# Conv stage in phases a step apart, 512-byte rows, gates in the combine: a two-layer convolution network on one NeuronCore

## Chip, cores and metric

The kernel runs on one core of a Trainium2 chip. The time is the device time of one execution in microseconds; the lower, the better. Times are given as the median of several runs. A profile is one more execution, recorded by the hardware profiler; its span runs from the first instruction to the last.

## The reference

The input x is 32 images of 128 channels and 56 x 56 pixels, float32. Two layers follow one another. What matters, cut from the reference:

```python
# layer 0: depthwise 7x7 conv, layernorm over channels, top-2 of 8 experts with capacity
x = conv_general_dilated(input, dw_kernel, (1, 1), ((3, 3), (3, 3)), feature_group_count=C) + dw_bias
x = transpose(x, (0, 2, 3, 1))
x = (x - mean) / sqrt(var + 1e-06) * ln_gamma + ln_beta      # over the 128 channels of a token
xf = x.reshape(T, C)                                         # T = 32*56*56 = 100352 tokens
topv, topi = top_k(xf @ Wg + bg, 2);  wts = softmax(topv)
order = argsort(-wts[:, 0])                                  # who gets a slot: sure tokens first
cap = int(1.25 * T / 8);  keep = pos < cap                   # 15680 slots per expert
h = gelu(einsum('ecd,edf->ecf', eb, W1) + b1)                # eb: the rows gathered into slots
y = einsum('ecf,efd->ecd', h, W2) + b2
contrib = y[slot] * gate;  moe = sum of a token's two contribs
x = input + x_skip + layer_scale * moe                       # x_skip = the normalised x
# layer 1: dilated 3x3 conv to 64 channels, gelu, 2-D FFT, attention over 8x8 channel blocks
# and a channel gate in frequency space, two inverse FFTs, absolute values, plus x
```

## The kernel before

A token is a pixel. Tokens are kept as 784 columns of 128 partitions: one column is two patches of 8 x 8 pixels, one of an image of the first half and one of the second. The program is written with a tile framework that gives out buffers, sets all semaphores and lays out the order of each engine's queue itself, by priority (the order of the program) and by what its model thinks is ready; each engine then runs its queue strictly in that order.

**Conv stage** (lines 114 to 286). Eight groups g of four images (two image pairs) each, 98 token columns a group. `conv(g, y)` gives 16 steps of eight channels: two loads on SP (xt, 784 KB; wt, 448 KB; three buffers each), 32 matrix products, and two VectorE evictions that add the bias and write y, a tile of 98 columns by 131 numbers (`ROW`: 128 channels, two gates, the first expert's number). There are two buffers of y. The evictions have two forms: L150 goes through the output token by token, L157 channel by channel. `norm(g, y)` gives seven steps of 14 columns and then `choose()`. A step takes the sum over channels (L172), the squares with an accumulator on ScalarE (L177, a column each), the root (L181) and reciprocal (L182), then two VectorE operations a column (L185, L188) that subtract the mean, scale, and apply gamma and beta in place; then TensorE transposes the columns four at a time (L196), ScalarE copies them out (L198), and a product per column with Wg (L200; the column is the stationary operand, Wg has 8 columns) gives the logits. `choose()` takes the two largest of eight logits for the 98 columns, the softmax, the sort key, writes the gates and the expert's number into the last three numbers of each row of y (L256 to L258), and issues seven stores of y to xf in DRAM on SP (L269, 917 KB each). The loop at L274 puts a norm step of group g-1 behind every second conv step of group g; the conv of group g+2 writes into the y buffer that group g's stores read.

**Selection and experts** (L305 to L684). A threshold on the key is found per expert by 24 bisections (count, L352), then lists of token numbers are made. `fetch` gathers 512 rows of xf (L585, GpSimd, 128 rows at a time, 524 bytes each), transposes them (L591), and works out each row's gate from its last three numbers with three small VectorE operations (L596, L604). `expert` does the two products (L619, L627) with Gelu between; VectorE adds the bias (L638), multiplies by the gate (L644), and SP stores the rows to yf.

**Layer 1** (L690 to the end). `layer1_input` prepares a pair of images in seven steps: load the normalised rows from xf (L738), gather each token's two expert rows from yf with 14 GpSimd gathers (L742, into four buffers of seven columns), add them (L748, twice), transpose, and add into the padded input (L758). The first pair is prepared before the loop; the steps of every further pair are put between the parts of the pair before by `ahead()`. In the loop: the 3x3 convolution (L837), Fourier transforms as pairs of transposes (L780, copied by VectorE, L781) and products (L793, L981), the attention weights (L872 to L894), the attention (L901 to L914) and the gate.

Of the kernel before, what the change touches and what calls it, by code (L numbers as in the profile page):

```python
# [55 lines left out]
ROW = C + 3  # L56
# [15 lines left out]
def conv_seq_kernel(ctx: ExitStack, tc: tile.TileContext, t: dict, out: bass.AP, dbg: dict):  # L72
# [9 lines left out]
    route = ctx.enter_context(tc.tile_pool(name="route", bufs=1))  # L82
    dram = ctx.enter_context(tc.tile_pool(name="dram", bufs=1, space=DRAM))
# [17 lines left out]
    xf = dram.tile([J * 128, ROW], F32, name="xf")  # L101
# [3 lines left out]
    slot1 = route.tile([128, J], I32, name="slot1")  # L105
    slot2 = route.tile([128, J], I32, name="slot2")
# [6 lines left out]

    with tc.tile_pool(name="a1", bufs=1) as a1, tc.tile_pool(name="a2", bufs=2) as a2, tc.tile_pool(
# [5 lines left out]
        wg = load(a1, "wg", [C, E], t["Wg"])  # L120
        bgB = load(a1, "bgB", [128, E], rowbc(t["bg"], 128))
        revi = load(a1, "revi", [128, E], rowbc(t["revi"], 128))
        TG = 2 * NP
        TC = 2 * NB

        def conv(g, y):


            def step(c0):
                xt = a3.tile([PK, CB, 4 * NCB * NB], F32, name="xt")  # L130
                nc.sync.dma_start(out=xt, in_=t["x8"][g, c0 // CB])
                wt = a3.tile([PK, CB, 2, P8 * P8], F32, name="wt")
                nc.sync.dma_start(out=wt, in_=t["wt"][c0 // CB])
                xv = xt.rearrange("k c (h n q) -> k c h n q", h=2, n=2)
                for c4 in range(0, CB, 4):
                    ps = bank("psa")
                    for c in range(4):
                        for b in range(2):
                            for h in range(2):
                                nc.tensor.matmul(  # L140
                                    ps[h * 64 : (h + 1) * 64, c * TG : (c + 1) * TG],
                                    lhsT=wt[:, c4 + c, b, :],
                                    rhs=xv[:, c4 + c, h, :, b * NB : b * NB + NP],
                                    start=(b == 0),
                                    stop=(b == 1),
                                )
                    yo = y[:, :, c0 + c4 : c0 + c4 + 4]
                    bias = dwbB[:, c0 + c4 : c0 + c4 + 4]
                    if c4 == 0:
                        nc.vector.tensor_tensor(  # L150
                            out=yo,
                            in0=ps[:, : 4 * TG].rearrange("p (c t) -> p t c", c=4),
                            in1=bias.unsqueeze(1).broadcast_to([128, TG, 4]),
                            op=ALU.add,
                        )
                    else:
                        nc.vector.tensor_tensor(  # L157
                            out=yo.rearrange("p t c -> p c t"),
                            in0=ps[:, : 4 * TG].rearrange("p (c t) -> p c t", c=4),
                            in1=bias.unsqueeze(2).broadcast_to([128, 4, TG]),  # L160
                            op=ALU.add,
                        )

            return [lambda c0=c0: step(c0) for c0 in range(0, C, CB)]

        def norm(g, y):

            lg = a2.tile([128, TG, E], F32, name="lg")

            def step(t0):  # L170
                s1 = a4.tile([128, TC], F32, name="s1")
                nc.vector.tensor_reduce(out=s1, in_=y[:, t0 : t0 + TC, :C], axis=AX.X, op=ALU.add)  # L172
                nc.vector.tensor_scalar(out=s1, in0=s1, scalar1=-1.0 / C, scalar2=None, op0=ALU.mult)  # L173
                ss = a4.tile([128, TC], F32, name="ss")
                for i in range(TC):
                    sq = a4.tile([128, C], F32, name="sq")
                    nc.scalar.activation(  # L177
                        sq, y[:, t0 + i, :C], AF.Square, bias=s1[:, i : i + 1], accum_out=ss[:, i : i + 1]
                    )
                sd = a4.tile([128, TC], F32, name="sd")  # L180
                nc.scalar.activation(sd, ss, AF.Sqrt, scale=1.0 / C, bias=eps6)  # L181
                nc.vector.reciprocal(sd, sd)  # L182
                for i in range(TC):
                    yi = y[:, t0 + i, :C]
                    nc.vector.scalar_tensor_tensor(  # L185
                        out=yi, in0=yi, scalar=s1[:, i : i + 1], in1=gB, op0=ALU.add, op1=ALU.mult
                    )
                    nc.vector.scalar_tensor_tensor(  # L188
                        out=yi, in0=yi, scalar=sd[:, i : i + 1], in1=bB, op0=ALU.mult, op1=ALU.add
                    )  # L190
                pl = bank("pl")
                for i0 in range(0, TC, 4):
                    ni = min(4, TC - i0)
                    pt = bank("pyt")
# [80 lines left out]
        for g in range(HI // 2):  # L275
            y = a2.tile([128, TG, ROW], F32, name="y")
            steps = conv(g, y)
            for i, step in enumerate(steps):
                step()
                if i % 2 and behind:  # L280
                    behind.pop(0)()
# [850 lines left out]
```

## Time and profile before

| what | value |
|---|---|
| time, median of 3 runs | 6373.91 us (6367.38 to 6375.63) |
| profiled execution | 6380.61 us, span 6378.8 us |
| TensorE, VectorE, ScalarE, GpSimd busy | 5121.9, 3203.4, 2190.9, 2595.7 us |
| conv stage | 0 to 1427 us |
| selection | 1427 to about 1724 us |
| experts | to about 3713 us |
| filling of layer 1 (first pair gathered) | to about 3880 us |
| layer 1, 16 pairs | to 6378.8 us |
| all DMA traffic | 622.42 MB |

A busy time is the sum over the engine's instructions without overlap. The share of a whole span says little here, since the five stages have different limits: what a change in a stage is worth is read from that stage's windows and from the chain of work that ended last, which is followed back from the last instruction. In the rows by line, "out<-in" are the program's tiles, the first number is the busy time, the second the mean length of one instruction, and behind the bar stands the engine's idle time in front of these instructions and what ended it. One matrix product in float32 shows as two passes, a transpose as one.

### The profile page before, as it was taken

To read this page: it belongs to the slowest core of one execution; us is meant where nothing else is said; L and a number is where in the kernel's file an instruction comes from. 1 tells how busy PE (TensorE), PEld (TensorE's weight loads), DVE (VectorE), ACT (ScalarE), POOL (GpSimd) and SP (SyncE) were. 2 spreads that over 40 slices of the span, in tenths; PEclk is the share of its full clock that TensorE was granted. 3 is DMA by queue.
4 is the path that set the end of the run, shared out by engine and by line. 5 is a ranking of instruction groups with operands and counts; after the bars stand their busy time and mean duration, and the time that the engine had idled before them with its cause. 6 is when DMAs were issued, how large, how long until landed. Compare 5 with 4: busy or idle time off the path is not lost.

```text
span 6378.8 us, 88000 instructions
## 1 busy us (share of the span) xinstructions
PE 5121.9 (80%) x33610; PEld 3637.3 (57%) x33610; DVE 3203.4 (50%) x7090; ACT 2190.9 (34%) x4455; POOL 2595.7 (41%) x2556
## 2 busy tenths in 40 slices
PE   7777877740299999999999937888888888888887
PEld 6666776630167667677777723555555555555554
DVE  4566665559753553553544323444444444444443
ACT  1333332330033333333333313444444444444444
POOL 0000000000154454454454457666666666666640
PEclk8666666655599999999999968888888899888888
DMA  7677776550022222222222243444444444444431
GB/s 206 149 168 161 158 159 155 118 95 23 12 69 66 65 66 69 64 68 68 66 66 67 69 119 73 108 107 106 106 107 107 106 108 106 105 107 106 108 91 26
DMA packets 515495, 622.42 MB, mean 98 GB/s; under 512 B 65529, under 2 KB 439810, under 8 KB 510978
## 3 DMA queue, kind: packets, MB, share of 16 engines
q1 hardware_dynamic: 433410, 448.14, 27.5%
q0 software_dynamic: 81664, 168.65, 12.4%
q8 instruction: 266, 4.36, 0.3%
q14 instruction: 155, 1.27, 0.1%
HBM read 448.37 MB, written 168.19 MB: 97 GB/s over the span
## 4 chain that ended last, share of the span: by engine, by line
PE 49%; DVE 14%; POOL 11%; issue 9%; DMA 8%; ACT 5%; SPq 3%; DVEq 0%; POOLq 0%; ACTq 0%
PE pf L837 12%; PE py L627 8%; POOL xg L585 7%; PE ph L619 6%; PE psa L140 5%; POOL y L742 5%; PE pl L200 4%; PE pm L793 3%; DVE junk L352 3%; SPq L269 3%; DMA xg<-xf,ids 2%; PE pyt L196 2%; PE pt L780 2%; DMA xf<-y 2%; DMA y<-yf,slot 1%
## 5 line engine op out<-in xcount | busy, mean ns | idle before, releaser
L585 POOL DMA_INDIRECT xg<-xf,ids x984 | 979.4, 995 | 2690.9 <-DVE ids L557 1720.4
L742 POOL DMA_INDIRECT y<-yf,slot x1568 | 1616.1, 1031 | 879.6 <-issue 433.9
L622 ACT ACTIVATE hT<-ph,b1t 128x512 f32<-128x512 f32 (+1 forms) x992 | 675.6, 682 | 1290.1 <-PE ph L619 1263.6
L627 PEld LDWEIGHTS py<-W,hT 128*128 128x128 f32 x7872 | 940.1, 192 | 220.8 <-issue 107.3
L627 PE MATMUL py<-W,hT 128*128 128x128 f32 x7872 | 987.1, 279 | 44.4 <-DVE yo L638 41.9
L619 PE MATMUL ph<-xT,W 128*128 128x512 f32 (+1 forms) x1984 | 886.5, 589 | 0.0
L837 PE MATMUL pf<-xp,cw 128*64 128x448 f32 x4032 | 782.1, 541 | 0.0
L140 PE MATMUL psa<-xt,wt 112*64 112x98 f32 x8192 | 556.9, 306 | 50.6 <-DMA wt<-in_wt_dram 49.9
L619 PEld LDWEIGHTS ph<-xT,W 128*128 128x128 f32 x1984 | 358.5, 191 | 348.6 <-issue 344.4
L140 PEld LDWEIGHTS psa<-xt,wt 112*64 112x64 f32 x8192 | 509.0, 178 | 73.3 <-issue 38.5
L837 PEld LDWEIGHTS pf<-xp,cw 128*64 128x64 f32 x4032 | 276.1, 135 | 444.8 <-issue 437.4
L596 DVE SCALAR_TENSOR_TENSOR gat<-xg 128x4 f32<-128x4 f32 (+2 forms) x256 | 42.2, 165 | 942.9 <-DMA xg<-xf,ids 942.1
L177 ACT ACTIVATE sq<-y,s 128x128 f32<-128x128 f32 x784 | 303.5, 391 | 284.6 <-DVE s L173 284.6
L748 DVE TENSOR_TENSOR xs<-xs,y 128x896 f32<-128x896 f32 x224 | 244.2, 1090 | 287.1 <-DMA y<-yf,slot 150.2
L196 PE MATMUL pyt<-ident,y 128*128 128x128 f32 x784 | 187.7, 371 | 235.2 <-DVE y L150 117.9
L200 PE MATMUL pl<-wg,yT 128*128 128x8 f32 x1568 | 326.8, 335 | 59.2 <-ACT yT L198 58.9
L200 PEld LDWEIGHTS pl<-wg,yT 128*128 128x128 f32 x1568 | 308.4, 291 | 111.3 <-ACT yT L198 93.5
L781 DVE COPY F<-pt 112x512 f32<-112x512 f32 x112 | 77.2, 690 | 511.6 <-PE pt L780 511.0
L198 ACT COPY yT<-pyt 128x512 f32<-128x512 f32 x224 | 118.5, 531 | 626.6 <-PE pyt L196 613.3
L844 ACT ACTIVATE feat<-pf,bn_shift,bn_scale 128x448 f32<-128x448 f32 x112 | 81.1, 724 | 703.9 <-PE pf L837 703.3
L196 PEld LDWEIGHTS pyt<-ident,y 128*128 128x128 f32 x784 | 137.3, 201 | 260.8 <-issue 126.3
L781 DVE COPY T<-pt 116x512 f32<-116x512 f32 (+3 forms) x368 | 234.3, 651 | 93.1 <-PE pt L780 91.2
(516 smaller groups left out, 7093.1 us busy)
## 6 DMA issues: line engine op xcount, KB each, us to landing
xt<-in_x_dram SPq DMA_DIRECT2D x128, 784.0 KB
yf<-yo SPq DMA_DIRECT2D x240, 256.0 KB
xp<-in_xp_dram SPq DMA_DIRECT2D x32, 1832.0 KB
wt<-in_wt_dram SPq DMA_DIRECT2D x128, 448.0 KB
xf<-y SPq DMA_DIRECT2D x56, 917.0 KB
xs<-xf SPq DMA_DIRECT2D x112, 448.0 KB
y<-yf,slot POOLq DMA_INDIRECT x1568
out_dram<-oa SPq DMA_DIRECT2D x224, 112.0 KB
```

The source lines that it names most:

```text
L140: nc.tensor.matmul(ps[h * 64 : (h + 1) * 64, c * TG : (c + 1) * TG], lhsT=wt[:, c4 + c, b, :], rhs=xv[:, c4 + c, h, :, b * NB : b * NB + N ...
L177: nc.scalar.activation(sq, y[:, t0 + i, :C], AF.Square, bias=s1[:, i : i + 1], accum_out=ss[:, i : i + 1])
L196: nc.tensor.transpose(pt[:, i * 128 : (i + 1) * 128], y[:, t0 + i0 + i, :C], ident)
L200: nc.tensor.matmul(pl[:, (i0 + i) * E : (i0 + i + 1) * E], lhsT=yT[:, i * 128 : (i + 1) * 128], rhs=wg, start=True, stop=True,)
L585: nc.gpsimd.indirect_dma_start(out=xg[:n, q, :], out_offset=None, in_=xf, in_offset=bass.IndirectOffsetOnAxis(ap=ids[:n, c0 + q : c0 + q + ...
L619: nc.tensor.matmul(ph[:, :ns], lhsT=W1[:, e, f * C : (f + 1) * C], rhs=xT[:, :ns], start=True, stop=True)
L622: nc.scalar.activation(hT[:, f, :ns], ph[:, :ns], AF.Gelu, bias=b1t[:, e, f : f + 1])
L627: nc.tensor.matmul(py[:n, q * C : (q + 1) * C], lhsT=hT[:, f, q * 128 : q * 128 + n], rhs=W2[:, e, f, :], start=(f == 0), stop=(f == FF // ...
L742: nc.gpsimd.indirect_dma_start(out=y[:, m, :], out_offset=None, in_=yf, in_offset=bass.IndirectOffsetOnAxis(ap=s[:, j0 + m : j0 + m + 1], ...
L748: nc.vector.tensor_tensor(out=xs, in0=xs, in1=y, op=ALU.add)
L781: copy(to[:, i0 : i0 + ni, :].rearrange("p i c -> p (i c)"), pt[: to.shape[0], : ni * 128],)
L837: nc.tensor.matmul(pf[i * DD : (i + 1) * DD, : 8 * W], lhsT=cw[:, k, :], rhs=xps[i][:, o : o + 8 * RP].rearrange("p (h w) -> p h w", w=RP) ...
```

## The change

It rewrites the conv stage and moves the gates.

- Rows of xf are 128 numbers, 512 bytes. The gates are kept in SBUF (`gates`, two tiles of 128 x 784) and no longer travel with the rows; the expert's number is not stored.
- Normalisation runs in blocks of 16 columns (six, and one of two). A block has five phases: `stats` (bn_stats per column on VectorE, seven small operations and one Sqrt), `norm` (one ScalarE Identity per column with a scale and a bias per partition, in place; then gamma and beta on VectorE for the whole block, and the block's store to xf, issued on ScalarE's queue), `across` (transposes and copies), `logits` (Wg, padded to 32 columns, as the stationary operand, and 512 tokens streamed; the four groups of four columns write four quarters of the partitions of one bank; a ScalarE copy), `back` (four transposes, and the bias).
- The phases of a block stand one conv step apart, and blocks start at steps 0, 1, 3, 4, 6, 7 and 9 of the next group's 16; `choose` follows at step 14 and issues no stores.
- All evictions have the token-by-token form.
- `fetch` and `expert` lose the gate operations; the combine multiplies each gathered tile of seven columns by its gate, on VectorE, before adding it.
- slot1 and slot2 are allocated after the conv stage.

```diff
-    xf = dram.tile([J * 128, ROW], F32, name="xf")
+    xf = dram.tile([J * 128, C], F32, name="xf")
+    gates = [route.tile([128, J], F32, name=f"gate{r}") for r in (1, 2)]
...
-                    if c4 == 0:
-                        nc.vector.tensor_tensor(
-                            out=yo,
...
+                nc.vector.tensor_tensor(
+                    out=y[:, :, cs],
+                    in0=ps[:, : 4 * TG].rearrange("p (c t) -> p t c", c=4),
+                    in1=dwbB[:, cs].unsqueeze(1).broadcast_to([128, TG, 4]),
+                    op=ALU.add,
+                )
...
+            def stats():
+                st = a2.tile([128, n, 6], F32, name="st", tag="st")
+                for i in range(n):
+                    nc.vector.bn_stats(out=st[:, i, :], in_=y[:, t0 + i, :])
+
+                me, mo, qe, qo = (st[:, :, i] for i in (1, 4, 2, 5))
+                df = a2.tile([128, n], F32, name="df", tag="df")
+                nc.vector.tensor_tensor(out=df, in0=me, in1=mo, op=ALU.subtract)
+                nc.vector.tensor_tensor(out=nb, in0=me, in1=mo, op=ALU.add)
+                nc.vector.tensor_tensor(out=sd, in0=qe, in1=qo, op=ALU.add)
+                nc.vector.scalar_tensor_tensor(
+                    out=df, in0=df, scalar=C / 4.0, in1=df, op0=ALU.mult, op1=ALU.mult
+                )
+                nc.vector.tensor_tensor(out=sd, in0=sd, in1=df, op=ALU.add)
+                nc.scalar.activation(sd, sd, AF.Sqrt, scale=1.0 / C, bias=eps6)
+                nc.vector.reciprocal(sd, sd)
+                nc.vector.scalar_tensor_tensor(
+                    out=nb, in0=nb, scalar=-0.5, in1=sd, op0=ALU.mult, op1=ALU.mult
+                )
+
+            def norm():
+                for i in range(n):
+                    yi = y[:, t0 + i, :]
                     nc.scalar.activation(
-                        sq, y[:, t0 + i, :C], AF.Square, bias=s1[:, i : i + 1], accum_out=ss[:, i : i + 1]
+                        yi, yi, AF.Identity, scale=sd[:, i : i + 1], bias=nb[:, i : i + 1]
                     )
...
+                for w, op in ((gB, ALU.mult), (bB, ALU.add)):
+                    nc.vector.tensor_tensor(
+                        out=yb, in0=yb, in1=w.unsqueeze(1).broadcast_to([128, n, C]), op=op
                     )
...
+                nc.scalar.dma_start(out=xfv[:, g * TG + t0 : g * TG + t0 + n, :], in_=yb)
...
+                def logits():
+                    pq = bank("plq")
+                    for k in range(4):
                         nc.tensor.matmul(
-                            pl[:, (i0 + i) * E : (i0 + i + 1) * E],
-                            lhsT=yT[:, i * 128 : (i + 1) * 128],
-                            rhs=wg,
+                            pq[32 * k : 32 * (k + 1), :],
+                            lhsT=wg,
+                            rhs=made["yT"][k],
+                            start=True,
+                            stop=True,
+                            tile_position=(0, 32 * k),
+                        )
+                    lq = made["lq"] = a2.tile([128, 512], F32, name="lq")
+                    nc.scalar.copy(lq, pq)
+
+                def back():
+                    pl = bank("pl")
+                    for i in range(4):
+                        nc.tensor.transpose(
+                            pl[:, i * 128 : (i + 1) * 128], made["lq"][:, i * 128 : (i + 1) * 128], ident
+                        )
...
-                nc.vector.tensor_copy(y[:, :, C + 2], firsts[0][:, cut])
...
-                for t0 in range(0, TG, TC):
-                    j0 = g * TG + t0
-                    nc.sync.dma_start(out=xfv[:, j0 : j0 + TC, :], in_=y[:, t0 : t0 + TC, :])
...
+            for b, n in enumerate(sizes):
+                for i, phase in enumerate(block(g, y, lg, t0, n)):
+                    at.setdefault(b * 3 // 2 + i, []).append(phase)
+                t0 += n
+            last = max(at)
+            at[last + 1] = [lambda: choose(g, lg)]
...
+            for k in range(NS):
+                conv(g, k * CB, y)
+                for phase in behind.pop(k, []):
+                    phase()
...
-            for n, q in spans(ns):
-                for to, i, op in ((gate, 0, ALU.is_equal), (gat2, 1, ALU.not_equal)):
-                    nc.vector.scalar_tensor_tensor(
...
-                nc.vector.tensor_tensor(
-                    out=yo[:n, q],
-                    in0=yo[:n, q],
-                    in1=gate[:n, q].unsqueeze(2).broadcast_to([n, nq, C]),
-                    op=ALU.mult,
-                )
...
+                nc.vector.tensor_tensor(
+                    out=y,
+                    in0=y,
+                    in1=gate[:, j0 : j0 + NB].unsqueeze(2).broadcast_to([128, NB, C]),
+                    op=ALU.mult,
+                )
                 nc.vector.tensor_tensor(out=xs, in0=xs, in1=y, op=ALU.add)
```

## The prediction

> **What bounds the kernel now.** I read first the chain that ended last, stage by stage in order of time, because the change touches three stages with different limits. In the conv stage (0 to 1427 us) it repeats one pattern; this is the end of the second group, columns start and length in us:
>
> ```profile
> 248.06 1.92 DVE s L172
> 250.96 1.92 DVE s L172
> 260.14 6.06 SPq L269
> 266.25 4.99 SPq L269
> 271.29 4.77 SPq L269
> 276.10 5.28 SPq L269
> 281.43 18.45 DMA xf<-y
> 302.41 1.88 PE pl L200 x8
> ```
>
> choose() ends, seven stores of xf are issued on SP, the last lands, and only then does the third group's convolution get its y buffer: from 260.1 to 302.4 nothing on the chain computes. The same mark (the first L200 after a store) stands at 302.4, 471.9, 639.8, 806.7, 976.4 and 1146.2, so a group takes 168.8 us. Group 0 takes 103 us with no normalisation beside it, group 7's convolution ends at 1262, and the first count (L352) starts at 1426.9, after a tail of 165 us.
>
> Next the busy times by window (length; PE, PEld, DVE, ACT, POOL; granted clock; DMA share; GB/s):
>
> ```profile
> 302.00:418.00 116.00, 104.52 (x1090) 94.75 (x1092) 68.31 (x184) 35.05 (x140) 0.00 (x0) 0.70 0.54 140
> 418.00:472.00 54.00, 23.15 (x235) 20.38 (x231) 33.55 (x96) 22.67 (x95) 0.00 (x0) 0.61 1.18 209
> 1262.00:1380.00 118.00, 68.18 (x294) 60.92 (x294) 81.41 (x245) 58.62 (x235) 0.00 (x0) 0.50 0.35 56
> 1380.00:1427.00 47.00, 0.00 (x0) 0.00 (x0) 11.07 (x21) 0.28 (x1) 0.00 (x0) 0.50 0.89 143
> 3000.00:3600.00 600.00, 587.21 (x3350) 425.69 (x3349) 264.18 (x631) 205.71 (x302) 296.89 (x299) 0.99 0.27 67
> ```
>
> The reader is to see that a group is 116 us in which TensorE is 90% busy, plus some 53 us in which it mostly waits; that the tail is a serial normalisation and then 47 us of store; and that the expert stage is TensorE at 98%, so nothing taken from VectorE there can be worth much. Last, the rows of the other stages:
>
> ```profile
> L627 PE MATMUL py<-W,hT 128*128 128x128 f32 x7872 | 987.1, 279 | 44.4 <-DVE yo L638 41.9
> L748 DVE TENSOR_TENSOR xs<-xs,y 128x896 f32<-128x896 f32 x224 | 244.2, 1090 | 287.1 <-DMA y<-yf,slot 150.2
> ```
>
> **Conv stage, what goes.** The xf store no longer waits for choose(); each block stores itself during steps 1 to 10 of the next group's 16, so y is free long before it is wanted and SP's loads no longer stand behind it. That removes the 260-to-302 pattern. What is late next is whichever engine has most work in a group. I price each, from the rows of 302 to 471.
>
> VectorE: the rows sum to 114 us (union by the windows 102). Out: L185 28.9, L188 28.4, L172 14.1, L173 1.2, L182 1.6, and L157's 16 at 840 ns. In: 98 bn_stats, which no row shows; bounds 0.2 us (128 elements at the 2.01 us that L172 takes for 1792, plus the 0.06 us of a bare memset) and 0.37 us (L872 with its accumulator read); I take L185's 0.295, the same shape, 28.9. Seven times six small operations at 0.17 (L173) and one reciprocal at 0.23: 8.8. Gamma and beta on 16 tiles at once: between L748 (896 elements, 1.09 us) and L323 (4096, 4.42 us) 2048 elements take 2.29, twelve of them and two small ones 28.3. All 32 evictions in L150's form, 558 ns: 17.9. choose() less two copies 15.1, L207's successor 1.9. Sum 101, times 102/114: 90 us (84 to 97 with the bounds).
>
> TensorE: L140 70.2, L196 23.2 and L200 39.9. L200 goes. In: 24 transposes back at 0.237, 5.7; per block of 16 eight passes of 512 columns, priced by L619's 0.447 (886.5 over 1984): if four column quarters run together 0.9, one after another 3.6, so 5 to 22; the two-tile block 0.8. Sum 105 to 121 at this group's clock (0.61 to 0.70). At the first group's 0.89, where 655 passes took 35.3 us instead of 44.9, it would be a fifth less: 82 to 95. I take 100.
>
> ScalarE: L177 was 37.9 plus 18.5 of accumulator reads; the Identity pass has no such read but a second pointer. Bounds 98 x 0.29 and 98 x 0.39; I take 38. The copies (25 at 0.53, and 6 of lq) 16, Sqrt and table loads 5: 59 us. The stores now sit on its queue, and in front of each it waits for two VectorE passes, 4.6 us. Queued behind are the next Sqrt and yT copies, for which VectorE and TensorE wait; that is the third rival.
>
> The Trainium skill speaks against this move: ScalarE: Activation LUTs, Rules for kernel authors, gives plain multiply and add to VectorE; by the fit in its section What ACT_TABLE_LOAD costs (186 ns, 93 for each pointer operand, 0.833 an element, 93 overlapping) a pass is estimated at 386 ns, 37.8 us a group, no different from the row. What the rule misses here is that VectorE is the fuller engine.
>
> DMA: loads 20.2 MB a group. Saturated in 10 to 95 us they ran at 273 GB/s: 74 us. The store: in the window 1384 to 1427 the 524-byte rows took 97.5% of 43 us for 6.7 MB, 160 GB/s. As 512-byte rows they are the shape of the expert stage's yf stores, which moved
>
> ```profile
> q1 hardware_dynamic: 114400, 56.74, 10.7%
> ```
>
> in 1850 to 3600, thus 56.74 MB in 187 us, 303 GB/s. So 21 to 40 us a group; I take the nearer row, 21. Sum 95 us (to 114).
>
> DMA: Bandwidth & Descriptors, Issuing engines are not separate DMA queues, warns that a second issuing engine saves only the issue time. The row agrees in part: by the rule only SP's 26 us of issue would be saved per group, by the chain the whole 42, since the store also starts earlier; the bytes stay.
>
> So three engines stand at 90 to 100. TensorE filled 90% of the unstalled stretch and 76% of the whole group; I take 0.82 for the fullest one, **122, rounded to 120 us a group**, bounds 105 (95 at 0.9) and 145 (121 at 0.83).
>
> Tail: VectorE without evictions, 90 - 16 = 74, and about 21 for filling and draining the five phases (three cross-engine hand-overs at each end, some 3 us each as in L196 to L207 at 1275 to 1287, clock 0.5): 95 us, bounds 80 and 120. The store lies inside it. Conv stage: 103 + 7 x 120 + 95 = 1038 against 1427, **-389 us**.
>
> **Expert stage.** Out: three 0.16 us gate operations and L644 (0.66) per chunk, and rows of xg 12 bytes shorter. TensorE hides all of it; what can come back is the 44.4 us in which it waited, nearly all for L638 behind this work. I take **-20**, bounds -42 and 0.
>
> **Combine.** In: 224 multiplies of the form of L748, 1.09 us. Fourteen are in the first image pair's fill, where each hides under the next gather (14 x 1.25 us of POOL a step) and only the last two show, 2 us. The other 210 are 229 us, 15.3 a pair. Cover: TensorE's convolution (two of seven steps a pair, as at 5119 and 5154, run while it is 100% busy) and 61 waits of L748 for xs, 134.9 us together, in which the multiply can run first. Without cover: the steps at 5024, 5044, 5091 and 5105, where TensorE waits for a T copy or for at_ (7.8 us before L892), and where POOL waits for a y buffer until L748 (218.8 us in all). Four steps of 2.2 less the part under xs: 6 a pair, **+90**, bounds 0 and 230.
>
> **Sum.** The profiled execution took 6380.6 us, its span 6378.8; it lies 6.7 above the median. 6380.6 - 389 - 20 + 90 = 6062, from the median 6373.9: **6055 us**. Its own range is 5960 to 6160.
>
> **Rivals.**
> (1) The engines overlap as well as DMA floors allow: 105 a group, tail 85, conv 923, -504; experts -40, combine +40: 5870. For it: group 0 kept DMA full throughout. Against: every before-group has hand-over gaps (L207 waits 32 us a group for L200). Chance 0.17.
> (2) Half the gain: the clock stays at 0.65 with quarters one after another, or the store stays at 160 GB/s; 143 a group, tail 110, conv 1214, -213; combine +150: 6311. Between it and my range the ground belongs to it too, 6160 to 6360. For it: clock 0.50 in the tail and 0.61 at the group's turn, both around transposes. Chance 0.21.
> (3) Slower: ScalarE's strict order becomes the bound. Each block holds it for the two passes (4.6 us) and a store issue of 3.7 (SP's 25.9 over seven); if a Sqrt of the next block then stands behind the hold, VectorE's stats wait and the next hold doubles: 16.6 x 7 = 116 on 59, 175 a group, conv 103 + 1225 + 110 = 1438, +11, combine +90, experts -20: 6455. It decides from 165 a group. Against: order on the queues is laid out with a whole step (7 us) between phases. Chance 0.10.
> (4) Nothing nets out, the stall returns as a wait for loads and combine takes the rest: within 0.2%, about 13 us, which is what a measurement of this kernel can tell from none. 0.02.
>
> Forecast 0.50. Faster by over 0.2%: 0.50 + 0.17 + 0.21 = 0.88; same 0.02; slower 0.10. The range 5890 to 6290 leaves out part of (1), the top of (2) and (3), 0.2 together.
>
> **What would show it.** Right: no stretch after choose() in which SP issues and TensorE idles; L200-like marks 115 to 130 us apart; first count near 1040; an xf store of 0.9 MB landing at over 250 GB/s; the expert window's 98% kept and its L638 wait below 44; the period of an image pair (now 156 us: 3880 to 6378.8 over 16) up by 6. Wrong: bn_stats over 0.4 us; ScalarE idle in front of its own store issues for more than 8 us; TensorE waiting for a quartered pass; a pair longer by 15 us, or by nothing.

## The result and the profile after

The changed kernel takes 6761.44 us (median of 4 runs, 6753.65 to 6769.47) beside 6370.65 us for the kernel before (4 runs, 6362.77 to 6375.63). The ratio is 1.0615, 95% interval 1.0596 to 1.0633: six per cent slower, where 6055 us had been forecast. The profiled execution has a span of 6767.7 us, 388.9 more than before. One execution of the fused kernel below came out longer, at a lower granted clock (5966.18 us at 0.846, the other three 5875.26 to 5886.47 us at 0.884 to 0.887), and its ratio is taken without it. Marks that stand in both traces split this difference by stage (us; the first count is the first bisection step of the selection; a pair is counted from the VectorE operation that makes gb, L872 before and L908 after, which comes once in each of the 16 pairs):

| stretch | before | after | difference | predicted |
| --- | --- | --- | --- | --- |
| start to the first count | 1426.8 | 1059.1 | -368 | -389 |
| from there to the issue of the last store of yf (3713.2, 3293.2) | 2286 | 2234 | -52 | -20 |
| from there to the first gb (3927.4, 3530.8) | 214 | 238 | +23 | +2 |
| 15 pairs, first gb to last (6279.3, 6669.8) | 2351.9 | 3139.0 | +787 | +88 |
| last gb to the end | 99.5 | 97.9 | -2 | 0 |

Both gains came about as forecast. The loss is the period of a pair, from 2351.9 / 15 = 156.8 us to 3139.0 / 15 = 209.3, where 6 us more had been forecast. The two rows that the period is read from, before and after (length in ns, then the start of the first and of the last in us):

```profile
L872 DVE SCALAR_TENSOR_TENSOR gb<-pg,ident x16: 281/284/291, 3927.4 to 6279.3; 128x128 f32<-128x128 f32 x16
```

```profile
L908 DVE SCALAR_TENSOR_TENSOR gb<-pg,ident x16: 283/284/292, 3530.8 to 6669.8; 128x128 f32<-128x128 f32 x16
```

These are the page's costliest groups that belong to it (busy time, mean ns of one, then the engine's idle time ahead of them and what ended it):

```profile
L772 POOL DMA_INDIRECT y<-yf,slot x1568 | 1583.4, 1010 | 1712.9 <-DVE xs L784 850.6
...
L778 DVE TENSOR_TENSOR y<-y,gate 128x896 f32<-128x896 f32 x224 | 244.8, 1093 | 1397.7 <-DMA y<-yf,slot 1301.5
...
L784 DVE TENSOR_TENSOR xs<-xs,y 128x896 f32<-128x896 f32 x224 | 243.4, 1090 | 100.0 <-DMA xs<-xf 96.9
```

The 224 multiplies of L778 are 244.8 us of work, at the duration that was forecast (1093 ns). What was not forecast is the 1397.7 us behind the bar: VectorE stood idle in front of them, 1301.5 us of it until a gather had landed. Before, the adds waited 150.2 us for gathers. GpSimd, in front of its gathers, now waits 850.6 us for the adds (before: 218.8), since an add sets a y buffer free. The waits of layer 1 alone, from 3600 to 6700 us (engine, line, what it waited for; us in total, times, longest), say the same:

```profile
DVE y L778 <- DMA y<-yf,slot: 1124.1, 181, 9.5
POOL y L772 <- DVE xs L784: 828.0, 62, 24.7
```

So each engine waits for the other. Why, the order of VectorE's queue shows; this is an excerpt of it (line, out<-in with the numbers of the tiles; the operations in between left out):

```
L778 y_23591<-y_23591,gate2      multiply of step k+1
L784 xs_23463<-xs_23463,y_23465  adds of step k
L784 xs_23463<-xs_23463,y_23475
L778 y_23725<-y_23725,gate1      multiplies of step k+2
L778 y_23735<-y_23735,gate2
L784 xs_23579<-xs_23579,y_23581  adds of step k+1
L784 xs_23579<-xs_23579,y_23591
```

A multiply needs its gathered tile and nothing of xs, and the framework has put it a step ahead of the add that uses it. The four buffers of y hold two steps. So the gathers of step k+2 can't begin before the adds of step k have set their buffers free, and the multiplies of step k+2 stand right behind these same adds. VectorE's timeline shows what comes of it (start, length, instruction, in brackets the idle time before it and what ended it):

```profile
5056.33 1.09 DVE L778 TENSOR_TENSOR y<-y,gate 128x896 f32<-128x896 f32 x1 [9.16 <-DMA y<-yf,slot]
5065.20 1.09 DVE L778 TENSOR_TENSOR y<-y,gate 128x896 f32<-128x896 f32 x1 [7.24 <-DMA y<-yf,slot]
...
5076.54 2.22 DVE L784 TENSOR_TENSOR xs<-xs,y 128x896 f32<-128x896 f32 x2 [1.38 <-DMA xs<-xf]
...
5089.14 1.09 DVE L778 TENSOR_TENSOR y<-y,gate 128x896 f32<-128x896 f32 x1 [6.44 <-DMA y<-yf,slot]
5097.97 1.09 DVE L778 TENSOR_TENSOR y<-y,gate 128x896 f32<-128x896 f32 x1 [6.67 <-DMA y<-yf,slot]
...
5110.37 1.08 DVE L784 TENSOR_TENSOR xs<-xs,y 128x896 f32<-128x896 f32 x1
```

From 5047.2 VectorE stood still for 9.16 us until the gather of the multiply at 5056.33 had landed, then 7.24 us for the next one. At 5076.54 come the adds of the step before, and behind them the multiplies of the following step, which wait 6.44 and 6.67 us. GpSimd's timeline has the other half:

```profile
5077.90 1.68 POOL L772 DMA_INDIRECT y<-yf,slot  x1 [14.66 <-DVE xs L784]
...
5111.73 1.08 POOL L772 DMA_INDIRECT y<-yf,slot  x1 [15.68 <-DVE xs L784]
```

Its next gather starts behind the add that frees the buffer, after 14.66 and 15.68 us of standing still. A tile is seven gathers 1.25 us apart, and VectorE mostly comes to a multiply while they are still being issued: by the two timelines three or four of the seven had started in 124 of the 224 cases, and all seven in 16. TensorE pays at once, since the copies and attention steps that it needs stand behind the multiplies on VectorE:

```profile
5103.99 1.93 PE L816 MATMUL pt<-ident,Q 128*116 128x128 f32 x8 [11.75 <-DVE Q L983]
```

The conv stage and the experts look as forecast. Windows (length; PE, PEld, DVE, ACT, POOL busy; granted clock; DMA share; GB/s), two of the conv stage and one of the expert stage:

```profile
300.00:420.00 120.00, 76.81 (x1201) 66.83 (x1198) 83.24 (x220) 59.40 (x140) 0.00 (x0) 0.83 0.80 225
420.00:540.00 120.00, 81.21 (x1162) 71.79 (x1164) 81.45 (x217) 58.91 (x139) 0.00 (x0) 0.77 0.81 216
1370.00:3280.00 1910.00, 1907.87 (x10962) 1385.69 (x10962) 634.46 (x1093) 674.58 (x987) 974.69 (x972) 1.00 0.25 68
```

In the conv stage the longest gap of TensorE at the turn of a group, 17.5 to 22.5 us before, is 9.5 to 13.8 us; the DMA engines are busy for 0.80 and 0.81 of the time, and the granted clock is 0.83 and 0.77 where 0.70 and 0.61 were read before. In the expert stage TensorE is busy for 1907.87 of 1910 us.

### The profile page after: what moved, and what is told of

The parts are those of the page before. It is cut to its first block, busy times and chain, and to the rows that moved or that the text cites. A ratio compares the mean times of both kernels' runs of the same rounds, so it can differ in the third digit from the quotient of the medians.

```text
span 6767.7 us, 83459 instructions
## 1 busy us (share of the span) xinstructions
PE 4931.3 (73%) x32650; PEld 3431.8 (51%) x32650; DVE 3033.5 (45%) x5826; ACT 2205.0 (33%) x3694; POOL 2572.0 (38%) x2556
## 3 DMA queue, kind: packets, MB, share of 16 engines
q10 hardware_dynamic: 101248, 51.38, 2.6%
## 4 chain that ended last, share of the span: by engine, by line
PE 32%; POOL 21%; issue 20%; DVE 8%; DMA 4%; ACT 1%; DVEq 0%; SPq 0%; POOLq 0%; ACTq 0%
POOL y L772 21%; PE py L663 14%; PE ph L655 12%; DVE junk L402 3%; DMA y<-yf,slot 2%; PE pxt L640 2%; DMA xs<-xf 1%; PE pm L829 1%; PE pf L873 1%; DVE xs L784 1%; DVE y L778 1%; PE pm L1017 0%; PE pg L862 0%; PE pt L816 0%; DVE xp L794 0%
## 5 line engine op out<-in xcount | busy, mean ns | idle before, releaser
L772 POOL DMA_INDIRECT y<-yf,slot x1568 | 1583.4, 1010 | 1712.9 <-DVE xs L784 850.6
L778 DVE TENSOR_TENSOR y<-y,gate 128x896 f32<-128x896 f32 x224 | 244.8, 1093 | 1397.7 <-DMA y<-yf,slot 1301.5
L674 DVE TENSOR_TENSOR yo<-py,b2t 128x512 f32<-128x512 f32 (+2 forms) x256 | 170.7, 669 | 1185.2 <-PE py L663 1185.2
L136 PE MATMUL psa<-xt,wt 112*64 112x98 f32 x8192 | 420.1, 265 | 83.0 <-DMA wt<-in_wt_dram 66.0
L136 PEld LDWEIGHTS psa<-xt,wt 112*64 112x64 f32 x8192 | 396.7, 148 | 121.6 <-issue 65.4
L196 PE MATMUL pyt<-ident,y 128*128 128x128 f32 x784 | 155.0, 378 | 302.6 <-DVE nb L174 150.9
L1004 ACT ACTIVATE ob<-pm 64x448 f32<-64x448 f32 x224 | 120.4, 538 | 642.3 <-DMA out_dram<-ob 469.2
L181 ACT ACTIVATE y<-y,nb,sd 128x128 f32<-128x128 f32 x784 | 310.8, 486 | 16.6 <-DVE nb L174 16.6
L144 DVE TENSOR_TENSOR y<-psa,dwbB 128x392 f32<-128x392 f32 x256 | 143.7, 564 | 322.4 <-PE psa L136 307.9
L784 DVE TENSOR_TENSOR xs<-xs,y 128x896 f32<-128x896 f32 x224 | 243.4, 1090 | 100.0 <-DMA xs<-xf 96.9
L829 PE MATMUL pm<-rh,T 112*128 112x116 f32 x928 | 165.2, 333 | 147.9 <-DVE T L817 147.9
```

Source lines behind the costliest of these rows:

```text
L136: nc.tensor.matmul(ps[h * 64 : (h + 1) * 64, c * TG : (c + 1) * TG], lhsT=wt[:, c4 + c, b, :], rhs=xv[:, c4 + c, h, :, b * NB : b * NB + N ...
L181: nc.scalar.activation(yi, yi, AF.Identity, scale=sd[:, i : i + 1], bias=nb[:, i : i + 1])
L196: nc.tensor.transpose(pt[:, i * 128 : (i + 1) * 128], y[:, t0 + i0 + i, :], ident)
L772: nc.gpsimd.indirect_dma_start(out=y[:, m, :], out_offset=None, in_=yf, in_offset=bass.IndirectOffsetOnAxis(ap=s[:, j0 + m : j0 + m + 1], ...
L778: nc.vector.tensor_tensor(out=y, in0=y, in1=gate[:, j0 : j0 + NB].unsqueeze(2).broadcast_to([128, NB, C]), op=ALU.mult,)
L784: nc.vector.tensor_tensor(out=xs, in0=xs, in1=y, op=ALU.add)
```

## The experiments

Each kernel was run once beside the kernel before on the same chip, except two that were timed in rounds. How far a single run can be trusted: one program that was run twice (stored late, below) had spans of 5814.7 and 5815.0 and its first count at 983.6 and 987.9. Six kernels with the same conv stage had the first count at 1051.2 to 1060.0, and seven with the same fused combine had pairs of 151.4 to 152.5 us.

**Six kernels on the combine.** Theory H: the multiply needs only the gathered tile, so it is put ahead of where the add stood, and VectorE, strictly in order, waits there. Theory T: it is VectorE's additional work. Theory C: it is something else of the change.

The fused version gives the same result with one operation per column, which needs xs as the add did:

```
-nc.vector.tensor_tensor(out=y, in0=y, in1=gate[...], op=ALU.mult)
-nc.vector.tensor_tensor(out=xs, in0=xs, in1=y, op=ALU.add)
+for m in range(NB):
+    nc.vector.scalar_tensor_tensor(out=xs[:, m, :], in0=y[:, m, :],
+        scalar=gate[:, j0 + m : j0 + m + 1], in1=xs[:, m, :], op0=ALU.mult, op1=ALU.add)
```

> The change with the multiply and the add of the combine in one operation per column (scalar_tensor_tensor: y times gate plus xs), so that nothing of it can start before the normalised rows xs have landed. Theory H (the multiply needs only the gather, is queued one step early, and VectorE, strictly in order, stands in front of it until the gather lands): an image pair returns from 209 us to 157 to 167 us, the wait for y at the combine falls from 1300 us to under 400, total 5950 to 6110 us. Theory T (the time of the multiply itself and the longer hold on the y buffers is the loss): VectorE still does 14 x 7 x 0.265 = 26 us a pair instead of 15 for the adds of before, so two thirds of the loss stay: a pair about 190 us, total about 6500. Theory C (the loss has nothing to do with the multiply, but with the 512-byte rows, the moved tiles or the loads): no change, 6700 to 6760.

Measured, in rounds: 5881.32 us (median of 4, 5875.26 to 5966.18), ratio to the kernel before 0.9178 (0.9145 to 0.921). A pair takes 152.3 us, less than the 157 to 167 that theory H gave.

```profile
L779 DVE SCALAR_TENSOR_TENSOR xs<-y,gate,xs 128x128 f32<-128x128 f32 x1568 | 452.8, 345 | 211.7 <-DMA y<-yf,slot 148.0
```

That is 452.8 us of work, nearly as much as the multiplies and adds of the change together (244.8 + 243.4 = 488.2), and yet the waits for gathers are 148.0 us, as in the kernel before (150.2). (A fused operation takes 452.8 / 1568 = 0.289 us; no row shows the 0.265 that theory T reckoned with.)

The second leaves the multiply out:

```
-nc.vector.tensor_tensor(out=y, in0=y, in1=gate[...], op=ALU.mult)
```

> The change with the multiply by the gates left out (both experts' rows are added with weight one). H and T: a pair takes 157 us as before, total 5930 to 5980; this is what the rest of the change is worth. C: a pair stays near 209 us, total over 6600.

Measured: 5983.8 us, a pair 158.3.

```profile
L778 DVE TENSOR_TENSOR xs<-xs,y 128x896 f32<-128x896 f32 x224 | 244.2, 1090 | 286.1 <-DMA y<-yf,slot 152.5
```

The third does this part alone: the kernel before, rows of 524 bytes and all, with only the gates taken from the experts to the combine:

```
+nc.vector.tensor_copy(gates[0][:, cut], w1)
+nc.vector.tensor_copy(gates[1][:, cut], w2)
...
-nc.vector.tensor_tensor(out=yo[:n, q], in0=yo[:n, q], in1=gate[:n, q]..., op=ALU.mult)
...
+nc.vector.tensor_tensor(out=y, in0=y, in1=gate[...], op=ALU.mult)
 nc.vector.tensor_tensor(out=xs, in0=xs, in1=y, op=ALU.add)
```

> The kernel before with only the gates moved into the combine (rows still 524 bytes, conv stage as it was, gate work of the experts taken out). H and T: a pair 205 to 212 us, total 7080 to 7170. C: a pair 157 to 165 us, total 6330 to 6480.

Measured: 7152.68 us, a pair 208.7.

```profile
L731 DVE TENSOR_TENSOR y<-y,gate 128x896 f32<-128x896 f32 x224 | 244.7, 1092 | 1390.1 <-DMA y<-yf,slot 1319.1
```

The loss needs nothing of the rest of the change: 208.7 beside 209.3, and the same 1.3 ms of waiting. Theory C falls. This kernel also settles a second point: its first count (1456.4) and its last store of yf (3690.2) are 2233.8 us apart, as in the changed kernel (2234), so the 52 us of the expert stage come with the gate operations taken out and not with the shorter rows.

The fourth keeps the 224 multiplies as they are and only holds them, in VectorE's order, behind a copy of one element of xs:

```
+if s is slot1:
+    hold = nc.vector.tensor_copy(touch, xs[:, 0, 0:1])
+with tc.issue_after(hold.ins):
     nc.vector.tensor_tensor(out=y, in0=y, in1=gate[...], op=ALU.mult)
```

> The change with the same 224 multiplies, only held in VectorE's order behind a one-element copy that reads xs, so that they stand where the adds stand. H: a pair 160 to 170 us, total 5980 to 6130, the wait in front of the multiply under 400 us. T: the same VectorE time and the same hold on the buffers, so a pair stays at 200 to 209 us, total over 6600. C: as T.

Measured: 5912.63 us, a pair 153.3, again less than theory H gave (160 to 170).

```profile
L772 POOL DMA_INDIRECT y<-yf,slot x1568 | 1708.7, 1090 | 743.1 <-issue 444.7
...
L782 DVE TENSOR_TENSOR y<-y,gate 128x896 f32<-128x896 f32 x224 | 240.0, 1084 | 117.8 <-DMA y<-yf,slot 111.4
...
L788 DVE TENSOR_TENSOR xs<-xs,y 128x896 f32<-128x896 f32 x224 | 242.0, 1085 | 2.2
```

The same 240 us of multiplying; its waits for gathers are down from 1301.5 to 111.4 us, GpSimd's idle time from 1712.9 to 743.1. With the work unchanged and its place alone moved, a pair loses 56.0 of its 209.3 us, a little more than the 52.5 that the change had added. Theory T falls, H stands.

The little more was a surprise: with the multiply a pair took 153.3, without it 158.3. A fifth kernel holds the adds alone:

```
 # no multiply
+with tc.issue_after(hold.ins):
     nc.vector.tensor_tensor(out=xs, in0=xs, in1=y, op=ALU.add)
```

> The changed kernel without the gates' multiply (left out: the scaling by the gates), and with both adds of a step put behind a one-element copy that reads xs. It splits the 158.3 us of a pair without the multiply from the 153.4 with the multiply held. Theory O (order alone: VectorE must not meet an operation that needs a gather before the step's xs has landed): a pair of 150 to 154 us, total 5880 to 5915, so that the multiply's 15 us a pair cost nothing at all. Theory V (the order is no better, and 158.3 against 153.4 is something else that the multiply brings): a pair of 157 to 159, total 5970 to 5990.

Measured: 5929.34 us, a pair 154.7, just outside what theory O gave (150 to 154, total 5880 to 5915).

```profile
L782 DVE TENSOR_TENSOR xs<-xs,y 128x896 f32<-128x896 f32 x224 | 244.2, 1090 | 139.4 <-DMA y<-yf,slot 122.7
```

Idle time in front of the adds falls from 286.1 to 139.4. Of the 5.0 us a pair between the two kernels, 3.6 are thus the order alone; for the other 1.4 no cause was shown, and it is little more than the 1.1 by which kernels with the same combine differ. The multiply itself, once held, costs nothing that these runs can see (153.3 with, 154.7 without).

A sixth asked whether one more y buffer lets GpSimd run far enough ahead:

```
+d8 = ctx.enter_context(tc.tile_pool(name="d8", bufs=5))
...
-y = d4.tile([128, NB, C], F32, name="y")
+y = d8.tile([128, NB, C], F32, name="y")
```

> The changed kernel, multiply as it was, with five buffers for the gathered y in place of four (a fifth is all that fits). Theory H (VectorE reaches the multiply before its gather has landed, because the multiply's only input is the gather): a fifth buffer lets GpSimd begin one gather earlier, so its waits for a buffer shrink by up to one multiply-to-add distance; a pair goes from 209.3 to 185 to 205 us, total 6400 to 6700, and the multiplies still wait over 700 us in all. Theory B (the four buffers alone make the loss): a pair of 155 to 165, total below 6100. If the loss doesn't depend on buffers: 209, 6760.

Measured: 6764.15 us, a pair 208.9: nothing. The expected 185 to 205 was wrong.

```profile
L779 DVE TENSOR_TENSOR y<-y,gate 128x896 f32<-128x896 f32 x224 | 244.8, 1093 | 1398.9 <-DMA y<-yf,slot 1338.7
```

In this kernel's queue on VectorE one multiply of step k+3 stands in front of the adds of step k+1, half a step further ahead than before: the order takes up what the buffer gives, and the ring stays closed. More than five buffers weren't tried.

**Five kernels on the conv stage**, all on the fused version, to judge the parts of the -368 us. First the rows, 516 bytes for 512, stored and gathered whole:

```
+ROW = C + 1
-xf = dram.tile([J * 128, C], F32, name="xf")
+xf = dram.tile([J * 128, ROW], F32, name="xf")
...
-y = a2.tile([128, TG, C], F32, name="y")
+y = a2.tile([128, TG, ROW], F32, name="y")
```

> The fused version with rows of xf one element longer, 516 bytes for 512, stored whole and gathered whole (the added column is zero). Theory S (the store hides beside engines that are fuller, whatever its rate): the first count within 20 us of 1059, total 5870 to 5905, with the store's rate falling from 292 to about 160 GB/s of engine time. Theory R (512-byte rows carry a good part of the conv stage's gain, as in the rival with half the gain): DMA goes from 95 to 114 us a group and more, the first count at 1150 or later, total 5975 or more.

Measured: 5916.98 us, the first count at 1102.5, between the two theories. The page's row of the store's queue (packets, MB, share of 16 engines), after:

```profile
q10 hardware_dynamic: 101248, 51.38, 2.6%
```

and with 516 bytes:

```profile
q10 hardware_dynamic: 101248, 51.79, 5.3%
```

By these, 51.38 MB in 2.6% of 6767.7 us are 292 GB/s, and 51.79 MB in 5.3% of 5915.2 us are 165 GB/s. A group goes from 122.0 to 128.2 us (five periods between choose()'s Exp operations, 944.74 - 334.54 and 987.55 - 346.52). The Trainium skill, DMA: Bandwidth & Descriptors, How a descriptor splits into AXI transactions, says that a row which doesn't start on a boundary of 256 bytes also fetches the bytes below its start. By its count of beats a 512-byte row costs 16 and a 516-byte row at a random start an estimated 20, which would leave about 230 GB/s; the 165 measured say that this is less than half of it.

Next the store as a whole, named at the end of the group on SP, as it stood before:

```
-nc.scalar.dma_start(out=xfv[:, g * TG + t0 : g * TG + t0 + n, :], in_=yb)
...
 # end of choose()
+for t0 in range(0, TG, 2 * NB):
+    nc.sync.dma_start(out=xfv[:, j0 : j0 + 2 * NB, :], in_=y[:, t0 : t0 + 2 * NB, :])
```

> The fused version with xf stored as before: seven transfers of 14 columns on SP, issued at the end of a group behind choose(). Statistics, ScalarE's normalising and the quartered logits stay. Theory W (the stall of some 42 us a group was most of the gain): each of seven turns costs 30 to 42 us again and the tail ends 15 to 25 us later, so the first count goes from 1059 to between 1285 and 1380 and the total to 6105 to 6200. Theory N (the cheaper work on the engines was most of the gain): the first count at 1100 to 1180, total below 6010.

Measured: 5816.51 us, the first count at 983.6: neither theory, but 75 us better. The reason is that this store isn't late. VectorE's timeline has the last pass over the first sixteen columns of a group,

```profile
452.88 2.26 DVE L185 TENSOR_TENSOR y<-y,bB 128x2048 f32<-128x2048 f32 x1
```

and SP's the first store:

```profile
455.22 0.38 SPq L304 DMA_DIRECT2D xf<-y  x1
```

The store leaves as the pass ends. No column of y is written by choose() any more, so nothing ties the store to it, and the order on the queue follows the data and not the place in the program. What this kernel really changed is the queue. That was tried by itself:

```
-nc.scalar.dma_start(out=xfv[:, g * TG + t0 : g * TG + t0 + n, :], in_=yb)
+nc.sync.dma_start(out=xfv[:, g * TG + t0 : g * TG + t0 + n, :], in_=yb)
```

> The fused version with xf still stored block by block, but issued on SP, between the loads, in place of ScalarE. With the store late on SP the first count stood at 983.6, with the store early on ScalarE at 1059.0, a group at 113.6 against 122.0 us. Theory A (the wait on ScalarE's queue, in front of each store, for two VectorE passes is what costs the 75 us): taking it off ScalarE gives most of it back, the first count at 980 to 1010, a group at 112 to 116. Theory E (it is the early transfer itself, its bytes or its place in VectorE's order, that costs): 1045 to 1075, a group at 120 to 124. If the loads that now stand behind a store on SP are late for it, more than 1075.

Measured: 5801.94 us, the first count at 978.5, a group 112.6 us ((880.21 - 317.36) / 5): theory A. How ScalarE's queue costs it is in the changed kernel's timeline of ScalarE:

```profile
474.91 0.31 ACT L172 ACTIVATE sd<-sd,eps 128x16 f32<-128x16 f32 x1 [0.28 <-DVE sd L171]
479.67 0.37 ACTq L188 DMA_DIRECT2D xf<-y  x1
480.86 0.59 ACT L198 COPY yT<-pyt 128x512 f32<-128x512 f32 x1 [5.65 <-PE pyt L196]
...
483.90 6.27 ACT L181 ACTIVATE y<-y,nb,sd 128x128 f32<-128x128 f32 x16
```

The root at 474.91 ends at 475.2. Next in the queue is the store of the block whose Identity passes ended at 474.4; it leaves at 479.67, when VectorE's two passes are done. Behind it stand the four copies of yT, and only behind those, at 483.90, the next block's sixteen Identity passes, though VectorE had their last operand (L174) at 480.06. With the store on SP the order is another:

```profile
453.73 1.26 ACT L181 ACTIVATE y<-y,nb,sd 128x128 f32<-128x128 f32 x3 [4.45 <-DVE nb L174]
454.90 0.56 ACT L198 COPY yT<-pyt 128x512 f32<-128x512 f32 x1
455.37 0.49 ACT L181 ACTIVATE y<-y,nb,sd 128x128 f32<-128x128 f32 x1
```

The passes begin as their operand comes, and the copies go in between. (By its bracket the first copy above had to wait for its transposes in any case; the passes had not.) The holds of the next two stores are shorter (1.1 and 3.2 us); by the timeline the stage's 56 stores stand behind some 115 us of idle ScalarE in all. How much of the cost is the hold and how much the order that came with it, these runs don't separate. The window 300 to 900 (the same columns as above) has the sum of it. The store on ScalarE:

```profile
300.00:900.00 600.00, 389.18 (x5834) 340.63 (x5834) 408.37 (x1088) 288.85 (x677) 0.00 (x0) 0.81 0.81 219
```

and on SP:

```profile
300.00:900.00 600.00, 405.13 (x6226) 356.36 (x6222) 448.83 (x1199) 299.51 (x717) 0.00 (x0) 0.83 0.85 227
```

In the same 600 us TensorE gets through 6226 passes in place of 5834. The prediction weighed a rule on this (the Trainium skill, DMA: Bandwidth & Descriptors, Issuing engines are not separate DMA queues): a second issuing engine saves issue time alone. Here it cost 80 us on balance. The queue that issues is held until the data is ready, which the rule does not speak of.

A further kernel put choose() behind the 16th step, where the kernel before has it:

```
-at[last + 1] = [lambda: choose(g, lg, y)]
+at[NS] = [lambda: choose(g, lg, y)]
```

> The fused version with the late store on SP, and with choose() put at the end of the next group's 16 steps, where the kernel before has it, in place of step 14. Theory P (the 42 us stall went because choose() and the store behind it now come before the end of the group, not because blocks store themselves): the stall comes back, the marks of choose() 135 to 160 us apart instead of 113.6, the first count at 1130 to 1310. Theory Q (the stall went because the cheaper work ends earlier than the loads anyway): marks at 113 to 118, the first count at 980 to 1010.

Measured: 5810.93 us, marks 114.5 us apart ((885.96 - 313.22) / 5), the first count at 985.5. For the same reason as above this says only that choose()'s place is of no matter. To tie the store to choose() indeed, the last kernel lets choose() write one channel of y back, unchanged:

```
+nc.vector.scalar_tensor_tensor(
+    out=y[:, :, 0], in0=w2, scalar=0.0, in1=y[:, :, 0], op0=ALU.mult, op1=ALU.add)
 for t0 in range(0, TG, 2 * NB):
     nc.sync.dma_start(...)
```

> In the three versions that name the store at the end of a group, SP's records show it leaving as soon as its columns are normalised (at 455.2, right behind the gamma and beta passes that end at 455.1), since nothing in it depends on choose() any more; so they are early stores on SP and say nothing about a late one. Here a neutral operation (w2 times 0 plus the first channel of y, written back) ties all of y, and with it the seven transfers on SP, to choose(), as the three columns written by choose() did in the kernel before. Theory W (that tie was the stall of 42 us): the marks of choose() go from 113 to 140 to 160 us apart, seven stores leave in a row, and the first count goes from 984 to 1180 to 1340; total 6010 to 6170. Theory N (the cheaper work made the room): marks below 122, first count below 1060, total below 5890.

Measured: 5820.92 us, marks 111.9 us apart ((877.62 - 318.16) / 5), the first count at 1002.1. The tie was there, as SP's timeline shows, seven stores in a row behind choose():

```profile
436.10 18.31 SPq L307 DMA_DIRECT2D xf<-y  x7
```

and still no group was longer; only the end grew: from the seventh mark to the first count 124.5 us pass, where the stored-late kernel took 98.4, and the first count comes 14 to 18 us later than in its two runs. Who waited for these stores, in us and times, first in the kernel before and then here:

```profile
  DVE y L150: 66.0, 5
```

```profile
  DVE y L144: 5.4, 3
```

Theory W falls: with rows of 512 bytes and the shorter work, the convolution asks for its buffer when the stores have all but landed. Which of the two makes the room wasn't tried; the seven issues take 18.0 to 19.6 us on SP, where they took 25.3 to 30.6 before. Nor was the tie tried together with choose() behind the 16th step: here choose() stands at step 14, and these two steps may be part of the room.

**The better version.** The fused combine with the store on SP (named at the end of the group, and leaving early) was timed in five rounds:

> The fused version with the late store on SP, timed in rounds (the same program as the one that stored late in a single look). From its single time of 5816.5 beside 6385.4: ratio 0.905 to 0.917 against the kernel before; against the fused version with the early store (0.9178 of before) about one per cent less.

Measured: 5811.04 us (5792.52 to 5816.74), ratio to the kernel before 0.9067, interval 0.9051 to 0.9084. It beats both kernels, and the fused version with the store on ScalarE (0.9145 to 0.921) as well. The version that names each block's store on SP was run once (5801.94 us), within this range.

## Why the prediction was wrong

**The combine, +90 (0 to 230): the step that failed.** It measured +810 (787 in the 15 pairs, 23 in the filling). The step read "61 waits of L748 for xs, 134.9 us together, in which the multiply can run first", and took its upper bound as 210 multiplies of 1.09 us. The duration was right (1093 ns) and the count was right. What was wrong is that running first was booked as cover. An operation that needs only the gather can be put a step ahead of the add on VectorE's queue, and it was; there it met a gather that the adds just ahead of it had only released, waited 1301.5 us in 16 pairs, and everything behind it waited too. The bound was made of work and had no room for a wait. The rows for a better bound were in the trace of before: a tile is seven gathers 1.25 us apart, so an operation that meets a gather just begun waits an estimated 8.75 us (the longest wait in layer 1 was 9.5), and 14 of them a pair some 122 us; 81 (1301.5 / 16) were waited and 52.5 showed. That the waiting, and not the work, is the cause is shown by the held kernel (153.3 us a pair with the same 224 multiplies), and that it needs nothing else of the change by the kernel before with the gates alone moved (208.7).

That VectorE works its queue strictly in order is stated in the Trainium skill too (PSUM — Partial Sum Buffer, Engine vs sequencer instructions), and the timeline agrees with waits of 9.16 and 7.24 us in which VectorE ran nothing of what stood behind. The prediction asked this question of ScalarE's stores and not of its own new operation on VectorE.

**The conv stage, -389: -368 measured.** The period of a group was put at 120 us and is 122.0; first group and tail together came to 205 us (1059.1 - 7 x 122.0) for 198. Single terms, predicted and read: bn_stats 28.9 us a group and 20.4 (163.2 / 8; one record's median is 281 ns, but records overlap); the Identity passes 38 us a group and 38.9 (310.8 / 8); VectorE 90 us and 83 in a window of 120; DMA 95 and 96 (0.80 of 120); TensorE 100 and 77 to 81, since the granted clock rose to 0.8 and the quarters ran side by side. The store was taken at 303 GB/s and ran at 292. The 120 were worked out from TensorE as the fullest engine, 100 at 0.82; the fullest was DMA with 96, so that they came out so near is in part luck. Though the sum was right, its first reason was not. The stall was to go because the store no longer waits for choose(); with that tie put back, at step 14, it didn't return. The 42 us a turn, read from the chain, were not all standing still, either: TensorE's longest gap at a turn was 17.5 to 22.5 us, and VectorE waited for the stores 66.0 us in five turns, 13 in each. What the runs do show of the -368: rows of 512 bytes for 516 are worth 43 us of it (with the store on ScalarE), and the queue chosen for the store cost 80. How the rest divides between the shorter work on VectorE and TensorE and its spreading in phases was not taken apart, and stays open.

**The experts, -20 (-42 to 0): -52.** TensorE's waits in front of L627 went from 44.4 us to 2.1, and those few that transposes had had (3.7) with them. Taking the gates' work off VectorE paid in full, where about half had been taken, and beyond the stated bound of -42; some 6 us of the 52 are left without a row.

**The rivals.** The slower one named ScalarE's strict order as the mechanism. It was there (a hold of 4.5 us where 4.6 was said), but at 9 us a group (122.0 against 112.6) and not 55, so it only made the gain smaller. The mechanism that decided the sign was on no list: its sign, "a pair longer by 15 us", stood among the signs of error, without a price. With the wait put right, the two other large terms hold in sum, -409 forecast and -420 measured, because the conv stage fell 21 us short and the experts went 32 beyond, which is luck. The fused version at 0.9178 of the kernel before is 0.9178 x 6373.9 = 5850 us beside the 6055 that had been forecast; of the 205 between them 90 are the combine's term and 68 are 15 pairs that the fused form makes 4.5 us shorter than before; the rest was not taken apart.

## What to carry to other kernels

When an operation is added, ask first what it waits for and where it then lands in its engine's queue, and only then how long it takes: one that depends on fewer inputs than its neighbour can be put earlier than the neighbour and hold the whole engine there. Fuse it into the operation that consumes its result, or order it behind the input that arrives last. The same holds for a transfer: issue it on a queue whose engine has nothing else to do while the data is being finished (here SP's in place of ScalarE's, 80 us).

## What was not expected of the hardware

Rows of 516 bytes stored at 165 GB/s and rows of 512 bytes at 292: four bytes took 43% of the rate. A pass of 512 columns on 32 columns of the array has a median of 617 ns by its record, and yet a block's eight together took only 1.15 us (55.4 us over 48 blocks). One after another, at the 0.447 us a pass that L619 took, an estimated 3.6 us would have gone by, so the four quarters do run at the same time. And more work was faster than less: 452.8 us of fused operations gave a pair of 152.3 us, 244.2 us of bare adds one of 158.3.
